# A two-layer graph convolution on one core: blocks of nodes that begin at the node of a fixed edge, and own rows moved at row numbers from registers

## The chip, the cores and the metric

The kernel runs on one core of a Trainium2 chip. TensorE (PE in the profile) multiplies, VectorE (DVE) and ScalarE (ACT) work on elements, GpSimd (POOL) issues the indirect DMAs, and SyncE (SP) issues all other DMAs. The metric is the time of one execution in microseconds (us); lower is better.

## The reference

There are N = 6250 nodes with D = 512 features each and E = 100000 edges, sorted by destination. With h = relu(layer_norm(x)):

```python
deg  = segment_sum(1, src)
dinv = where(deg > 0, 1 / sqrt(deg), 0)
conv(h, W0, W1, b) = h @ W0 + segment_sum(h[src] * (-dinv[src] * dinv[dst]), dst) @ W1 + b
h1  = conv(relu(layer_norm(x)), W1_0, W1_1, b1)
h1  = leaky_relu(layer_norm(h1, gamma, beta), 0.01)
out = x + conv(h1, W2_0, W2_1, b2)
```

All is float32. The costly part is the sum over edges: for each edge a row of 2 KB is fetched by its source's number, and the rows are added up by destination.

## The kernel before, in words

**Start.** The node rows (49 blocks of 128, the last one of 106) are loaded in eight groups. DVE makes one-hot tables of the source numbers (L215), PE counts them (L221), and this gives each node's degree and dinv. From the layer norm's statistics and dinv come scales (`sc`, L260 and L261); ACT (L270) and DVE (L266, L268) turn the rows into dinv * relu(layer_norm(x)), and eight stores on SP's queue write them to a table in DRAM, `tab[0]` (L272). The edges' numbers are turned on PE so that a chunk of 128 edges is a column: `sidx` holds the sources as integers in SBUF (L287), `dl` the destinations as floats in PSUM (L283).

**Main part (`usual_path`).** PE's and POOL's orders are written out by hand; the other engines' orders come from a scheduler. Two layers run one after the other. POOL's only work is `gather` (L315): one indirect DMA per chunk fetches the 128 source rows into one of R = 44 ring slots `zr`. There are 782 chunks, so 782 gathers a layer. A gather waits until the slot's last reader, 44 chunks back, is done, and until the gather eight before it has landed; each block's gathers stand in POOL's order before that block's other work, up to 44 chunks beyond the block's first.

For each block of 128 nodes:

- `own` (L326) loads the block's own rows `xt` from x by SP; in layer 0 ACT makes h from them with the columns `rs_all` and `nb_all`, in layer 1 h is loaded from `h_tab`. PE turns h (`hT`) and multiplies it by W0 (`start_products`).
- `sums` (L349) does the sum over edges. The edges are sorted but where a node's edges begin is not known when the program is built. So `chunk_ranges` gives each quarter of 32 nodes a range of chunks wide enough for the spread of the edges' positions, up to 12 chunks. DVE compares the chunks' destinations with the nodes (`sel`, one instruction, L367), and PE multiplies each chunk's 128x32 selection with its gathered rows (L378). The four quarters write to four groups of 32 columns of the array and run side by side: one step `s` of the loop over four quarters is called a round here. The profile counts two PE instructions for each of these products. The blocks of a layer have 544 rounds and 2170 products.
- ACT scales the sums by -dinv (`agg`, L381), PE turns them (L322) and multiplies by W1 (L439).
- `finish` (L384): in layer 0 a layer norm and the leaky relu, and stores of dinv * h1 to `tab[1]` (L409) and of h1 to `h_tab` (L413); in layer 1 the sum with x and the store to out (L391).

Layer 1's first gather waits for all stores to `tab[1]`. In layer 0 ACT also counts the edges that the selections hold (`held`, `n_seen`, L370). If at the end some edge was not seen, `general_path` computes all anew in another way; with the inputs used here all 100000 edges are seen, and it does not run.

The program prints here the functions that the change touches:

Of the kernel before, what the change touches and what calls it, by code (L numbers as in the profile page):

```python
# [8 lines left out]
F32 = mybir.dt.float32  # L9
# [7 lines left out]
POOL = mybir.EngineType.Pool  # L17

P = 128
# [3 lines left out]
LOADED = 8  # L23
# [10 lines left out]
def chunk_ranges(N, E):  # L34


    NC = -(-E // P)
    res = []
    for b in range(-(-N // P)):
        ends = [min(N, b * P + q * Q) for q in range(NQ + 1)]  # L40
        m = max(math.ceil(SPREAD * math.sqrt(E * (n / N) * (1 - n / N)) / P) for n in ends)
        res.append([(max(0, ends[q] * E // (N * P) - m),
                     min(NC, -(-ends[q + 1] * E // (N * P)) + m)) for q in range(NQ)])
    return res
# [3 lines left out]
def gnn_kernel(  # L48
# [26 lines left out]

    nc = tc.nc
# [10 lines left out]
    ranges = chunk_ranges(N, E)  # L87
    NK = max(hi - lo for r in ranges for lo, hi in r)
# [9 lines left out]
    tab = [dram.tile([NB * P, D], F32, name=f"tab{i}") for i in range(2)]  # L98
    h_tab = dram.tile([NB * P, D], F32, name="h_tab")
# [7 lines left out]
    sdinv = const.tile([P, NB], F32, name="sdinv")  # L107
    rs_all = const.tile([P, NB], F32, name="rs_all")
    nb_all = const.tile([P, NB], F32, name="nb_all")
# [5 lines left out]
    n_seen = const.tile([P, NQ * NB], F32, name="n_seen")  # L115
# [9 lines left out]
    nc.sync.dma_start(src_i, src.rearrange("(p j) -> p j", j=EJ))  # L125

# [54 lines left out]
    nc.gpsimd.memset(n_seen, 0.0)  # L181


    nm_all = ep.tile([P, NB], F32, name="nm_all")
# [54 lines left out]
    with tc.tile_pool(name="fold", bufs=1) as dp, tc.tile_pool(  # L239
        name="fold_ps", bufs=1, space=bass.MemoryType.PSUM  # L240
    ) as dps:
        deg = dps.tile([P, NB], F32, name="deg")
        each = ident.rearrange("k (n s) -> k s n", s=2)
        for t in range(2):
            for i in range(2):
                nc.tensor.matmul(deg[t * LO : (t + 1) * LO, :], each[:, i, :], both[:, :, t, i],
                                 start=(i == 0), stop=(i == 1))
        root = dp.tile([P, NB], F32, name="root")
        some = dp.tile([P, NB], F32, name="some")
        nc.vector.tensor_scalar_max(root, deg, 1.0)  # L250
        nc.scalar.activation(root, root, AF.Sqrt)
        nc.vector.tensor_single_scalar(some, deg, 0.0, op=OP.is_gt)
        nc.vector.reciprocal(root, root)
        nc.vector.tensor_mul(dinv, root, some)
        nc.vector.tensor_scalar_mul(ndinv, dinv, -1.0)
        nc.vector.tensor_scalar_mul(sdinv, dinv, SLOPE)


        sc = dp.tile([P, 2, NB], F32, name="sc")
        nc.vector.tensor_mul(sc[:, 0, :], rs_all, dinv)  # L260
        nc.vector.tensor_mul(sc[:, 1, :], nb_all, dinv)  # L261
        for (i0, n), t in zip(groups, xs):
            for j in range(n):
                i = i0 + j
                if i % 2:
                    nc.vector.tensor_scalar(t[:, j, :], t[:, j, :], sc[:, 0, i : i + 1], sc[:, 1, i : i + 1],  # L266
                                            op0=OP.mult, op1=OP.add)
                    nc.vector.tensor_scalar_max(t[:, j, :], t[:, j, :], 0.0)  # L268
                else:
                    nc.scalar.activation(t[:, j, :], t[:, j, :], AF.Relu, bias=sc[:, 1, i : i + 1],  # L270
                                         scale=sc[:, 0, i : i + 1])
            nc.sync.dma_start(tab[0][i0 * P : (i0 + n) * P, :].rearrange("(i p) d -> p i d", p=P), t)  # L272


    with tc.tile_pool(name="turn", bufs=1) as wp, tc.tile_pool(
        name="turn_ps", bufs=2, space=bass.MemoryType.PSUM
    ) as wps:
        for t, res in zip(chunks, (dl, sidx)):
            f = wp.tile([P, NG, P], F32, name="f", bufs=2)
            nc.vector.tensor_copy(f, t)  # L280
            for g in range(NG):
                if res is dl:
                    nc.tensor.transpose(dl[:, g * P : (g + 1) * P], f[:, g, :], ident)  # L283
                else:
                    fT = wps.tile([P, P], F32, name="fT")
                    nc.tensor.transpose(fT, f[:, g, :], ident)
                    nc.scalar.activation(sidx[:, g * P : (g + 1) * P], fT, AF.Copy)  # L287
# [4 lines left out]
    n_unseen = nc.values_load(unseen[0:1, 0:1], min_val=0, max_val=E,  # L292
                              skip_runtime_bounds_check_because="a count of edges")
# [5 lines left out]
def usual_path(tc, have):  # L299
    nc = tc.nc  # L300
    (x, out, rows, tab, h_tab, sidx, dl, iota_r, w_sb, ident, eps, ones, dinv, ndinv, sdinv, rs_all, nb_all,
     bias1, bias2, gam, bet, n_seen, unseen, ranges, NK, N, E, D, NB, NC, KD) = (
        have[n] for n in ("x out rows tab h_tab sidx dl iota_r w_sb ident eps ones dinv ndinv sdinv rs_all "
                          "nb_all bias1 bias2 gam bet n_seen unseen ranges NK N E D NB NC KD").split())
    R = 44
    with ExitStack() as es:
# [5 lines left out]
        seen = 0  # L312
# [13 lines left out]
        def own(layer, b):  # L326

            r = rows[b]
            xt = pool.tile([P, D], F32, name="xt")
            if r < P:  # L330
                nc.vector.memset(xt, 0.0)
            for lo, hi in parts(r):
                nc.sync.dma_start(xt[lo:hi], x[b * P + lo : b * P + hi, :])
            h = pool.tile([P, D], F32, name="h")
            if layer == 0:
                nc.scalar.activation(h, xt, AF.Relu, bias=nb_all[:, b : b + 1], scale=rs_all[:, b : b + 1])  # L336
            else:
                nc.sync.dma_start(h, h_tab[b * P : (b + 1) * P, :])
            ps, hT = transposed(h, "hT")
            nc.scalar.activation(hT, ps, AF.Copy)  # L340
            if layer == 1 and b == NB - 1:
                nc.vector.tensor_add(xt, xt, bias2)
# [6 lines left out]
        def sums(layer, b):  # L349
            nonlocal seen  # L350
            rng = ranges[b]
            sel = pool.tile([P, NQ, NK, Q], F32, name="sel")
            node = pool.tile([P, NQ, Q], F32, name="node")
            nc.scalar.activation(node, iota_r.rearrange("p (q c) -> p q c", c=Q), AF.Copy, bias=float(b * P))
            n = rng[0][1] - rng[0][0]
            step = rng[1][0] - rng[0][0]
            if all(rng[q] == (rng[0][0] + q * step, rng[0][1] + q * step) for q in range(NQ)):
                dl0 = dl[:, rng[0][0] : rng[0][0] + 1]
                parts = [(sel[:, :, :n, :], node[:, :, None, :].to_broadcast([P, NQ, n, Q]),
                          bass.AP(tensor=dl0.tensor, offset=dl0.offset,  # L360
                                  ap=[dl0.ap[0], [step, NQ], [1, n], [0, Q]]))]
            else:
                parts = [(sel[:, q, : hi - lo, :], node[:, q, None, :].to_broadcast([P, hi - lo, Q]),
                          dl[:, lo:hi, None].to_broadcast([P, hi - lo, Q]))
                         for q, (lo, hi) in enumerate(rng)]
            for o, i, d in parts:
                nc.vector.tensor_tensor(o, d, i, op=OP.is_equal)  # L367
                if layer == 0:
                    held = pool.tile([P, NQ, NK, Q], BF, name="held")
                    nc.scalar.activation(held[:, : o.shape[1], : o.shape[2]] if len(o.shape) == 4  # L370
                                         else held[:, 0, : o.shape[1], :], o, AF.Copy,
                                         accum_out=n_seen[:, seen : seen + 1])
                    seen += 1
            ps = psum.tile([P, D], F32, name="ps")
            for s in range(NK):
                for q, (lo, hi) in enumerate(rng):
                    if lo + s < hi:
                        nc.tensor.matmul(ps[q * Q : (q + 1) * Q, :], sel[:, q, s, :], zr[(lo + s) % R],  # L378
                                         start=(s == 0), stop=(lo + s == hi - 1))
            agg = pool.tile([P, D], F32, name="agg")  # L380
            nc.scalar.activation(agg, ps, AF.Copy, scale=ndinv[:, b : b + 1])  # L381
            return agg

        def finish(layer, b, v, xt):  # L384
            if layer == 1:
                o = pool.tile([P, D], F32, name="o")
                if b < NB - 1:
                    nc.vector.tensor_add(v, v, bias2)  # L388
                nc.vector.tensor_add(o, v, xt)  # L389
                for lo, hi in parts(rows[b]):  # L390
                    nc.sync.dma_start(out[b * P + lo : b * P + hi, :], o[lo:hi])  # L391
# [13 lines left out]
            di = dinv[:, b : b + 1]  # L405
            t = pool.tile([P, D], F32, name="t")
            nc.scalar.activation(t, v, AF.Copy, scale=sdinv[:, b : b + 1])  # L407
            nc.vector.scalar_tensor_tensor(t, v, di, t, op0=OP.mult, op1=OP.max)  # L408
            nc.sync.dma_start(tab[1][b * P : (b + 1) * P, :], t)  # L409
# [3 lines left out]
            nc.sync.dma_start(h_tab[b * P : (b + 1) * P, :], g)  # L413

        for layer in range(2):
            w0, w1 = w_sb[2 * layer + 1], w_sb[2 * layer]
            t = 0
            for b in range(NB):
# [9 lines left out]
                if b + 1 < NB:  # L428
                    next_xt, hT = own(layer, b + 1)
                agg = sums(layer, b)  # L430
                if b + 1 < NB:
# [4 lines left out]
                if b + 1 < NB:  # L436
# [5 lines left out]
            if layer == 0:  # L442
# [4 lines left out]
                nc.vector.tensor_scalar(unseen, all_ps[0:1, 0, 0:1], -1.0, float(E), op0=OP.mult, op1=OP.add)  # L447
# [318 lines left out]
```

## Time and profile before

| | before |
|---|---|
| median of 10 runs | 2125.45 us (2124.57 to 2128.2) |
| the profiled execution's own time | 2125.43 us |
| its span | 2123.6 us |
| PE busy | 1912.3 us (90%) |
| POOL busy | 1481.9 us (70%) |
| DVE, ACT busy | 622.6 us, 413.8 us |
| gathers (L315) | 1564, mean 946 ns |
| mean granted TensorE clock | 0.977 |
| mean DMA rate | 245 GB/s |

The profile is one execution. It lists groups of instructions with their busy time, the mean of one and the engine's idle time before them, with what ended it; the waits between engines; the instructions in order of time; and, for any stretch of time, each engine's busy time, the granted clock of PE and the share of time that the 16 DMA engines were busy. An engine can be busy most of the time and still not be what sets the end.

### The profile page before, as it was taken

The numbers are of one execution on the slowest core, as the hardware profiler recorded it, in microseconds if no ns is written. First come the engines' busy times: TensorE is split into PE (matmuls) and PEld (weight loads), VectorE is DVE, ScalarE is ACT, GpSimd is POOL, SyncE is SP. The second block draws the span as 40 slices with busy tenths as digits, with TensorE's granted clock in tenths as the row PEclk, the third lists the DMA queues.
The fourth block names the chain that finished last, engine by engine and source line by source line (L and its number), as shares of the span: only waits on it lengthen the run. The fifth ranks groups of instructions, "written<-read, shape, count | busy, mean of one in ns | idle before, by whom it ended". The sixth has DMA issues, their size and how long they took to land. (4 is left out here: it accounts for less than half of the span.)

```text
span 2123.6 us, 28647 instructions
## 1 busy us (share of the span) xinstructions
PE 1912.3 (90%) x11456; PEld 698.3 (33%) x11456; DVE 622.6 (29%) x824; ACT 413.8 (19%) x811; POOL 1481.9 (70%) x1577
## 2 busy tenths in 40 slices
PE   4358999999999999999886989999999999999896
PEld 4222333333333333333321323333333333333332
DVE  8913333333333333333231211111111112112111
ACT  8622222222222222222210000000000000000000
POOL 0047777777777777777756777777777777777774
PEclk9869999999999999999997999999999999999999
DMA  9488788888888888887866788788788787887884
GB/s 328 153 281 255 240 255 247 248 254 247 249 256 245 251 254 244 252 255 242 252 211 206 238 256 255 240 256 250 246 255 252 243 256 243 252 255 244 251 250 146
DMA packets 184811, 521.08 MB, mean 245 GB/s; under 512 B 30235, under 2 KB 31797, under 8 KB 184666
## 3 DMA queue, kind: packets, MB, share of 16 engines
q0 software_dynamic: 125120, 410.09, 64.4%
q1 hardware_dynamic: 59546, 109.04, 14.3%
q8 instruction: 92, 1.51, 0.3%
q14 instruction: 53, 0.43, 0.1%
HBM read 467.68 MB, written 51.34 MB: 244 GB/s over the span
## 5 line engine op out<-in xcount | busy, mean ns | idle before, releaser
L315 POOL DMA_INDIRECT zr<-tab,sidx x1564 | 1478.9, 946 | 617.8 <-issue 264.5
L378 PE MATMUL ps<-zr,sel 128*32 128x512 f32 x8680 | 1091.5, 602 | 113.8 <-DMA zr<-tab,sidx 109.6
L378 PEld LDWEIGHTS ps<-zr,sel 128*32 128x32 f32 x8680 | 280.8, 110 | 853.2 <-issue 449.7
L367 DVE TENSOR_TENSOR sel<-dl,node 128x1536 f32<-128x1536 f32 (+5 forms) x110 | 160.8, 1471 | 883.8 <-PE ps L378 866.3
L347 PE MATMUL u_ps<-w,hT 128*128 128x512 f32 x784 | 380.4, 608 | 1.8 <-ACT hT L340 1.8
L439 PE MATMUL u_ps<-w,aT 128*128 128x512 f32 x784 | 354.3, 595 | 1.6 <-DVE aT L435 1.6
L381 ACT ACTIVATE agg<-ps,ndinv 128x512 f32<-128x512 f32 x98 | 67.3, 687 | 937.5 <-PE ps L378 937.5
L439 PEld LDWEIGHTS u_ps<-w,aT 128*128 128x128 f32 x784 | 149.4, 191 | 189.7 <-issue 187.4
L347 PEld LDWEIGHTS u_ps<-w,hT 128*128 128x128 f32 x784 | 134.1, 191 | 178.7 <-issue 176.3
L340 ACT ACTIVATE hT<-hT_ps 128x512 f32<-128x512 f32 x98 | 58.5, 597 | 503.1 <-PE hT_ps L322 503.0
L393 DVE TENSOR_TENSOR u_ps<-u_ps,bias 128x512 f32<-128x512 f32 x49 | 34.3, 699 | 217.7 <-PE u_ps L439 217.7
L388 DVE TENSOR_TENSOR u_ps<-u_ps,bias 128x512 f32<-128x512 f32 x48 | 33.6, 699 | 214.1 <-PE u_ps L439 214.1
L435 DVE COPY aT<-aT_ps 128x512 f32<-128x512 f32 x98 | 67.7, 691 | 79.0 <-PE aT_ps L322 79.0
L370 ACT ACTIVATE held<-sel 128x1536 bf16<-128x1536 f32 (+5 forms) x55 | 68.9, 1254 | 46.9 <-DVE sel L367 46.9
L221 PE MATMUL both_ps<-hi,lo 125*128 125x196 bf16 x400 | 39.3, 254 | 42.8 <-DVE hi L215 42.7
L322 PE MATMUL hT_ps<-ident,h 128*128 128x128 f32 x392 | 59.3, 274 | 16.6 <-ACT h L336 16.6
L322 PEld LDWEIGHTS hT_ps<-ident,h 128*128 128x128 f32 x392 | 49.2, 142 | 67.5 <-issue 67.5
L322 PEld LDWEIGHTS aT_ps<-ident,agg 128*128 128x128 f32 x392 | 48.9, 141 | 54.2 <-issue 50.4
L322 PE MATMUL aT_ps<-ident,agg 128*128 128x128 f32 x392 | 58.9, 273 | 1.7 <-ACT agg L381 1.7
L221 PEld LDWEIGHTS <-lo 125*128 125x128 bf16 x400 | 35.9, 100 | 46.0 <-issue 34.4
L408 DVE SCALAR_TENSOR_TENSOR t<-u_ps,dinv,t 128x512 f32<-128x512 f32 x49 | 36.8, 750 | 37.0 <-ACT t L407 37.0
L407 ACT ACTIVATE t<-u_ps,sdinv 128x512 f32<-128x512 f32 x49 | 33.7, 687 | 64.1 <-DVE u_ps L403 64.1
(74 smaller groups left out, 531.6 us busy)
## 6 DMA issues: line engine op xcount, KB each, us to landing
zr<-tab,sidx POOLq DMA_INDIRECT x1564
xt<-in_x_dram SPq DMA_DIRECT2D x96, 256.0 KB
tab<-t SPq DMA_DIRECT2D x49, 256.0 KB
h_tab<-g SPq DMA_DIRECT2D x49, 256.0 KB
h<-h_tab SPq DMA_DIRECT2D x49, 256.0 KB
out_dram<-o SPq DMA_DIRECT2D x48, 256.0 KB
tab<-xs SPq DMA_DIRECT2D x6, 1792.0 KB
xs<-in_x_dram SPq DMA_DIRECT2D x5, 1792.0 KB
```

Source lines behind the costliest of these rows:

```text
L221: nc.tensor.matmul(both_ps, hot[0][:, j, :], hot[1][:, j, :], start=(g == 0 and j == 0), stop=(g == EJ // (2 * GJ) - 1 and j == GJ - 1))
L315: nc.gpsimd.indirect_dma_start(out=zr[t % R], out_offset=None, in_=tab[layer], in_offset=bass.IndirectOffsetOnAxis(ap=sidx[:, t : t + 1], ...
L322: nc.tensor.transpose(ps[:, kc, :], h[:, kc * P : (kc + 1) * P], ident)
L340: nc.scalar.activation(hT, ps, AF.Copy)
L347: nc.tensor.matmul(u_ps, hT[:, kc, :], w0[:, kc, :], start=(kc == 0), stop=False)
L367: nc.vector.tensor_tensor(o, d, i, op=OP.is_equal)
L370: nc.scalar.activation(held[:, : o.shape[1], : o.shape[2]] if len(o.shape) == 4 else held[:, 0, : o.shape[1], :], o, AF.Copy, accum_out=n_ ...
L378: nc.tensor.matmul(ps[q * Q : (q + 1) * Q, :], sel[:, q, s, :], zr[(lo + s) % R], start=(s == 0), stop=(lo + s == hi - 1))
L381: nc.scalar.activation(agg, ps, AF.Copy, scale=ndinv[:, b : b + 1])
L408: nc.vector.scalar_tensor_tensor(t, v, di, t, op0=OP.mult, op1=OP.max)
L435: nc.vector.tensor_copy(aT, aT_ps)
L439: nc.tensor.matmul(u_ps, aT[:, kc, :], w1[:, kc, :], start=False, stop=(kc == KD - 1))
```

## The change

Blocks of a layer no longer begin at multiples of 128 nodes. `block_plan` chooses a fixed step of 1888 edges; block b begins at the node after that of edge b * 1888 - 1, read from dst at run time (`begin_i`, one DMA of 51 single numbers), the first at node 0, the last at node N - 128. So a block's edges lie at chunk numbers known far better, and a quarter's range is 4 to 7 chunks where it was up to 12. There are 53 blocks instead of 49, with 357 rounds and 1246 products a layer instead of 544 and 2170. A block loads, computes and stores 128 rows; those from the next block's begin on (`owned`, 106 to 128 rows are its own with the inputs used here) get no sums and are overwritten by the next block, whose stores come later. All 100000 edges are again seen.

As a block's rows begin anywhere, the per-node scales are no longer columns in SBUF: rs, nb and dinv are turned on PE, copied by ACT (`all_sb`) and stored to a table `scales` in DRAM, and each block in layer 0 loads its 128x3 scales as single 4-byte numbers (`sb`) and DVE makes two more from them (`sn`). Own rows, h, the scales and all stores are moved at row numbers that SP loads into registers, eight blocks at a time (`values_load_multi_w_load_instructions`). The selection is made by four compares, one a quarter, against `node`, which one ACT and one DVE instruction make from `first` and `owned`. `astray` counts blocks that own fewer than 0 or more than 128 nodes.

The diff, cut to its core:

```diff
+    n = math.ceil((E - deg * P) / (deg * P - SPREAD * sd(P)))
+    step = 16 * math.ceil((E - deg * P) / (16 * n))
...
+    tab = [dram.tile([n, D], F32, name=f"tab{i}") for i, n in enumerate((NB * P, N))]
+    h_tab = dram.tile([N, D], F32, name="h_tab")
+    scales = dram.tile([3, NB * P], F32, name="scales")
...
+    nc.sync.dma_start(begin_i[:, 1 : BL - 1],
+                      bass.AP(tensor=dst.tensor, offset=dst.offset + step - 1, ap=[[1, 1], [step, BL - 2]]))
...
+    all3 = ep.tile([P, 3, NB], F32, name="all3")
+    rs_all, nb_all = all3[:, 0, :], all3[:, 1, :]
...
-        nc.vector.tensor_scalar_mul(sdinv, dinv, SLOPE)
+        nc.vector.tensor_copy(all3[:, 2, :], dinv)
...
+    nc.vector.tensor_scalar(begin[:, 1 : BL - 1], begin_i[:, 1 : BL - 1], 1.0, float(N - P), op0=OP.add, op1=OP.min)
...
+    nc.vector.tensor_copy(first_i, begin[:, :BL])
+        nc.tensor.matmul(first_ps, ones[0:1, :], begin, start=True, stop=True)
+        nc.vector.tensor_scalar_add(first, first_ps, 1.0)
+        all_ps = fps.tile([NB, 3, P], F32, name="all_ps")
+        for k in range(3):
+            nc.tensor.transpose(all_ps[:, k, :], all3[:, k, :], ident)
+        all_sb = ep.tile([NB, 3, P], F32, name="all_sb")
+        nc.scalar.activation(all_sb, all_ps, AF.Copy)
+        nc.sync.dma_start(scales.rearrange("k (b p) -> b k p", p=P), all_sb)
+    nc.vector.tensor_sub(owned, first[:, 1:], first[:, :BL])
...
 def own(layer, b):
+            if b % LOADED == 0:
+                n = min(LOADED, BL - b)
+                _, vals = nc.values_load_multi_w_load_instructions(
+                    first_i[0:1, b : b + n], engines=(SP,), min_val=0, max_val=N - P,
+                    skip_runtime_bounds_check_because="held to the last block above")
+                for k in range(n):
+                    row[b + k] = bass.ds(vals[k], P)
-            for lo, hi in parts(r):
-                nc.sync.dma_start(xt[lo:hi], x[b * P + lo : b * P + hi, :])
+            nc.sync.dma_start(xt, x[row[b], :])
             if layer == 0:
-                nc.scalar.activation(h, xt, AF.Relu, bias=nb_all[:, b : b + 1], scale=rs_all[:, b : b + 1])
+                nc.sync.dma_start(sb[:, b, :], scales[:, row[b]].rearrange("k p -> p k"))
+                nc.vector.tensor_tensor(sn[:, b, :], sb[:, b, 2:3].to_broadcast([P, 2]), signs, op=OP.mult)
+                nc.scalar.activation(h, xt, AF.Relu, bias=sb[:, b, 1:2], scale=sb[:, b, 0:1])
             else:
-                nc.sync.dma_start(h, h_tab[b * P : (b + 1) * P, :])
+                nc.sync.dma_start(h, h_tab[row[b], :])
...
 def sums(layer, b):
+            nc.scalar.activation(plain, iota_r, AF.Identity, bias=first[:, b : b + 1])
+            nc.vector.scalar_tensor_tensor(node, iota_r, owned[:, b : b + 1], plain, op0=OP.is_lt, op1=OP.mult)
+            for q, (lo, hi) in enumerate(rng):
+                wide = [P, hi - lo, Q]
+                nc.vector.tensor_tensor(sel[:, at[q] : at[q + 1], :], dl[:, lo:hi, None].to_broadcast(wide),
+                                        node[:, None, q * Q : (q + 1) * Q].to_broadcast(wide), op=OP.is_equal)
...
-            for s in range(NK):
+            for s in range(max(hi - lo for lo, hi in rng)):
                 for q, (lo, hi) in enumerate(rng):
                     if lo + s < hi:
-                        nc.tensor.matmul(ps[q * Q : (q + 1) * Q, :], sel[:, q, s, :], zr[(lo + s) % R],
+                        nc.tensor.matmul(ps[q * Q : (q + 1) * Q, :], sel[:, at[q] + s, :], zr[(lo + s) % R],
                                          start=(s == 0), stop=(lo + s == hi - 1))
-            nc.scalar.activation(agg, ps, AF.Copy, scale=ndinv[:, b : b + 1])
+            nc.scalar.activation(agg, ps, AF.Copy, scale=sn[:, b, 0:1])
...
 def finish(layer, b, v, xt):
-                for lo, hi in parts(rows[b]):
-                    nc.sync.dma_start(out[b * P + lo : b * P + hi, :], o[lo:hi])
+                nc.sync.dma_start(out[row[b], :], o)
...
-            nc.sync.dma_start(tab[1][b * P : (b + 1) * P, :], t)
+            nc.sync.dma_start(tab[1][row[b], :], t)
...
-            nc.sync.dma_start(h_tab[b * P : (b + 1) * P, :], g)
+            nc.sync.dma_start(h_tab[row[b], :], g)
```

In the built program the row-number DMAs keep their places in SP's order, each with a register instruction ahead of it; the two DVE instructions on `begin` and `first_i` stand before the first one-hot table, the copy `all_sb` stands on ACT ahead of the scaling of the rows, the store to `scales` stands on SP behind the eight stores to `tab[0]`, and the first gather waits for it too, because its ring slots reuse the memory of `all_sb`. POOL's order of gathers is the same.

## The prediction

> **What bounds the kernel now.** I read the page's first and fifth parts first: PE is busy 90% of the span, and its largest group, the rounds of L378, is what the change cuts.
>
> ```profile
> PE 1912.3 (90%) x11456; PEld 698.3 (33%) x11456; DVE 622.6 (29%) x824; ACT 413.8 (19%) x811; POOL 1481.9 (70%) x1577
> ...
> L315 POOL DMA_INDIRECT zr<-tab,sidx x1564 | 1478.9, 946 | 617.8 <-issue 264.5
> L378 PE MATMUL ps<-zr,sel 128*32 128x512 f32 x8680 | 1091.5, 602 | 113.8 <-DMA zr<-tab,sidx 109.6
> ```
>
> Then I asked whether the other candidate, POOL, ever rests. In the view of stretches of time, for L315 alone (busy us, count, PE's clock, DMA share, GB/s), each full 100 us holds the same work:
>
> ```profile
> 220.00:320.00 100.00, 75.63 (x81) 1.00 0.81 250
> 1000.00:1100.00 100.00, 75.62 (x81) 1.00 0.82 250
> 1600.00:1700.00 100.00, 75.63 (x81) 1.00 0.80 250
> ```
>
> 75.63 / 0.946 is 79.9 gathers in 100 us: one every 1.251 us, 0.946 busy and 0.30 between. The view of waits says the same (us in total, times, longest):
>
> ```profile
> PEld ps L378 <- DMA zr<-tab,sidx: 391.6, 431, 5.8
> POOL zr L315 <- issue: 264.5, 868, 0.3
> ...
> POOL zr L315 <- DMA zr<-tab,sidx: 134.6, 442, 0.3
> ...
> POOL zr L315 <- PE ps L378: 60.6, 199, 0.3
> ```
>
> Whatever POOL is said to wait for, it waits 0.3 us and never longer. The ring's first gathers, issued when PE does nothing, keep the same pitch. PE waits for the gathers, up to 5.8 us at a time. So the gathers' issue is the bound, and PE only nearly another. The span is a sum of five pieces: start to 125.27; 782 gathers, 781 x 1.251 = 977 us, to 1101.81; a turn between the layers of 21.16 us to 1122.97; 976 us to 2099.29; and the end, 24.3 us. 125.3 + 976.5 + 21.2 + 976.3 + 24.3 = 2123.6, the span. Its own time, 2125.43, is 1.8 us more, and the median is 2125.45.
>
> So only start, turn and end can move the span. In order of time (start, us, engine), the turn's first gather, then the end:
>
> ```profile
> 1122.97 0.94 POOL L315 DMA_INDIRECT zr<-tab,sidx  x1 [20.22 <-DMA tab<-t]
> ```
>
> ```profile
> 2099.29 0.95 POOL L315 DMA_INDIRECT zr<-tab,sidx  x1 [0.30 <-issue]
> ...
> 2102.31 1.07 PE L378 MATMUL ps<-zr,sel 128*32 128x512 f32 x8 [0.41 <-DMA zr<-tab,sidx]
> 2103.89 3.64 PE L378 MATMUL ps<-zr,sel 128*32 128x512 f32 x26 [0.52 <-DMA zr<-tab,sidx]
> ...
> 2109.83 5.40 PE L439 MATMUL u_ps<-w,aT 128*128 128x512 f32 x8 [0.79 <-DVE aT L435]
> ```
>
> and the start, where the scaled rows are stored:
>
> ```profile
> 87.14 17.74 ACT L270 ACTIVATE xs<-xs,sc 128x512 f32<-128x512 f32 x25 [1.21 <-DVE sc L261]
> ...
> 88.55 22.78 SPq L272 DMA_DIRECT2D tab<-xs  x8
> ```
>
> **The change part by part.** *The gathers* stay 2 x 782, in the same order: 0. Their cover against PE: a block now has 6.74 rounds (357 / 53). Products run in groups of up to four quarters, two passes each, 0.43 us a pass (the end's 26 instructions are one group of four and three of three: 8 passes in 3.64 us with the last one's full 0.59). So a round is 0.86 us, and a block's four other PE groups take (380.4 + 354.3 + 59.3 + 58.9) / 98 = 8.70 us. 6.74 x 0.86 + 8.70 = 14.5 us, against 782 / 53 x 1.251 = 18.46 us of gathers. The 374 rounds removed and the 8 block visits added (374 x 0.86 - 8 x 8.70 = 252 us of PE) lie beside POOL and buy nothing, unless at the ends.
>
> *DVE and ACT per block.* Four compares of 800 elements in all, by the rows of 1024 (1.223 us) and 256 (0.415): 0.146 + 1.05 ns an element, so 1.43 us against 1.76 now; two small ones (under 0.4) and one more ACT copy (0.3, as L354's). Both engines are idle for over half of a block: 0. DVE's `sn` waits for `sb`, with that block's compares behind it, but SP issues `sb` blocks ahead, right behind `xt`; at the start six `sn` stand ahead of the third block's compares, which PE needs some 35 us after the first gather. SP's extra DMA (0.32 us) and register instructions a block have 18 us: 0.
>
> *Own rows.* Three times 256 KB a block, 39 GB/s in a block's 20 us, become 8% more: 0. Layer 1's first h loads must now wait for the last `h_tab` store, as any row may be in it. Behind them stand PE's first transposes, and the round that needs chunk 11, which is issued 13.8 us after layer 1's first gather. Store, load (some 2 us each, as 1120.16 to 1122.97) and 8 products at half clock fit: 0.
>
> *The narrow loads.* `sb` is 384 numbers a block, 24 for each DMA engine. The trace has no 4-byte data. At 37.4 to 41 us mostly 512-byte packets kept all engines busy at some 42 ns each; the gathers' packets take 175 ns (64.4% of 16 engines over 125120). At 42 ns, 1.0 us an engine; at 175, 4.2. Of 18.46 us 19% is idle, 3.5 us. So 0 at 42, the nearest size, and (4.2 - 3.5) x 53 = +37 at 175, which I keep as a rival. The Trainium skill, "DMA: Bandwidth & Descriptors", Specifications, speaks against this load: below 512 bytes a DMA does read-modify-write. It gives no price per number, so by it the sum lies somewhere between my two ends; no row here shows it.
>
> *Start.* (a) Two DVE instructions stand ahead of the one-hot chain; small ones take 0.15 to 0.18 us: +0.3. If DVE has to wait for the 51 numbers, all 40 one-hots queue behind: up to +1.5. (b) ACT must copy `all_sb` before its 25 scalings, and that waits for three transposes. Four at half clock took 1.08 us (as at 127.93), a copy of 512 elements 0.60: 0.8 + 0.45, less 0.1 that the last `sc` took beside it: +1.15, between 0.5 and 2. The eight stores wait for these scalings, and DMA is full from 92 to 122 us (share 1.03), so they shift whole. (c) The first gather waits for the `scales` store too, 147 rows of 512 bytes: 0.4 us if spread over 16 engines, 6 on one; the load of 125 rows at 1 to 3 us kept only two tenths of the engines busy, so I take 21 rows on an engine, 0.85. Sum +2.3, bounds +0.9 and +9.
>
> *The turn and the end.* After chunk 781 lands, its group and three more ran, 3.64 us, as the last block's quarters ranged over 8, 8, 8 and 4 chunks. Now they range over 7, 7, 6 and 6: the group that holds chunk 781 holds the last two other products, and none follows. A lone group takes 1.07 (the row of 8 instructions). -2.57, twice. The out store of the block before, issued at 2098.57, moved beside the last gathers (4.60 us from issue to use; 3.85 at the turn, where no store did). It now comes some 1 us earlier: -0.2 (0 to -0.75). At the turn, the block before now ends its sums earlier and its store to `tab[1]` meets the last gathers: +0.6 (0 to +0.75, the difference of the two landings). Layer 1's first gather waits on three semaphores for ten: -0.1 (0 to -0.6).
>
> *The clock.* PE drops to half for 3.41 us after a stretch that it was half idle (busy us of PE first, clock behind the bracketed numbers):
>
> ```profile
> 2106.80:2110.21 3.41, 1.77 (x11) 0.72 (x6) 0.69 (x1) 0.69 (x1) 0.00 (x0) 1.00 0.01 2
> 2110.21:2113.62 3.41, 3.41 (x5) 1.33 (x4) 0.00 (x0) 0.00 (x0) 0.00 (x0) 0.50 0.02 7
> ```
>
> That cost the end 5.40 - 3.65 = 1.75 us, the turn nothing. With 4 us idle a block, PE will drop more often; one such stretch costs 1.7 us of PE, inside the 4. At each end I keep what is there: 0, bounds -1.75 and +1.75. The Trainium skill's "TensorE: Matmul & The Clock Gate", Part 1, names an idle window of about 3.4 us as the condition; the row shows a drop after a window 52% busy. By the page the end would run at full clock, 1.75 less, a sum of 2121.1; I go by the row.
>
> Sum: start +2.3; turn -2.57 + 0.6 - 0.1; end -2.57 - 0.2; in all -2.5. 2125.4 - 2.5 = **2122.9 us**.
>
> **The rivals.** *PE was the bound* (faster). For it: 90% busy. Then the 252 us would go, 1873. Against it: 0.3 us is POOL's longest wait for PE. Chance 0.02.
>
> *The ends gain more* (faster by over 4.25 us): the start costs only 0.9, the end keeps its clock, no store meets a gather: 0.9 - 5.14 - 0.6 - 0.75 - 1.75 = -7.3 at most, 2118.1; from 1.8 us below my sum on it decides. Chance 0.16.
>
> *The start delays more* (slower): the `scales` store on few engines, or a late `begin_i`; it decides from a start of +9.1 on, which my upper bounds just reach: 9.5 - 4.8 = +4.7, 2130.1. Chance 0.07.
>
> *The narrow loads fill the DMA engines* (slower). A gather waits for the one eight back, 10 us; landings take 3.9 to 4.6 now. Above 146 ns a number (3.5 / 24) the engines lack time and gathers come late: at 175 ns +37, 2161. Chance 0.05. That the blocks fail to cover the edges is excluded by the inputs.
>
> **How the numbers follow.** The likeliest case, the sum within 4.25 us of before, has 0.70; 0.2%, 4.25 us, is about what a measurement of this kernel tells from no change. Faster 0.16 + 0.02 = 0.18; slower 0.07 + 0.05 = 0.12; same 0.70. The range takes in the low end of the ends' case, 2118.5, and the start's, 2131; outside are PE as the bound, the narrow loads, and a little of both.
>
> **What would show it.** Right: L315 still 75.6 us in each 100; first gather near 127.5; turn near 19.1 us; PE busy some 80%, with a lower clock. Wrong: a pitch under 1.25 us, a POOL wait of over 0.3 us for gathers or PE within a layer, a first gather past 131.

## The result and the profile after

The changed kernel takes 2439.04 us (median of 9 runs, 2429.36 to 2453.12) against 2125.45 before: a ratio of 1.1482, 95% interval 1.1467 to 1.1497. It is slower, where no change to speak of was forecast. Its profiled execution took 2454.21 us, span 2452.4, so that all sums below go by 2452.4 against 2123.6, +328.8.

The page of the kernel after, first and fifth part:

```profile
PE 1714.8 (70%) x7957; PEld 628.1 (26%) x7957; DVE 652.5 (27%) x1353; ACT 420.7 (17%) x848; POOL 1483.2 (60%) x1578
...
L373 POOL DMA_INDIRECT zr<-tab,sidx x1564 | 1480.4, 947 | 913.1 <-PE ps L432 374.4
L432 PE MATMUL ps<-zr,sel 128*32 128x512 f32 x4984 | 789.5, 698 | 153.1 <-DMA zr<-tab,sidx 150.6
...
L380 PE MATMUL hT_ps<-ident,h 128*128 128x128 f32 x424 | 89.4, 350 | 479.1 <-DMA h<-h_tab 460.7
```

PE's rounds shrank as planned (1091.5 to 789.5 us busy), yet POOL's share of the span fell from 70% to 60%: it now rests. The last line is new: PE stood idle for 460.7 us ahead of the first transposes of a block, waiting for the load of h. Stretches of 100 us for the gathers alone (busy us, count, PE's clock, DMA share, GB/s) show where:

```profile
220.00:320.00 100.00, 75.62 (x81) 0.97 0.84 256
...
1600.00:1700.00 100.00, 56.29 (x60) 0.83 0.62 187
```

Layer 0 keeps the 75.6 us of before. Layer 1 does not. The five pieces of the span are: start to 125.89 (+0.6); layer 0's gathers 977.5 (+1.0); the turn 22.6 (+1.5); layer 1's gathers, 1126.00 to 2395.99, 1270.0 (**+293.7**); the end 56.4 (**+32.1**). The view of waits names the link (us in total, times, longest):

```profile
PE hT_ps L380 <- DMA h<-h_tab: 460.7, 52, 11.0
POOL zr L373 <- PE ps L432: 374.4, 269, 9.1
```

52 of the 53 blocks of layer 1, the layer in which h is loaded from DRAM, wait for it. PE falls behind, the ring of 44 chunks fills, and POOL waits for a free slot up to 9.1 us at a time. The chain that ended last, in one block of layer 1 (start, us, what):

```profile
1511.35 5.63 DMA h<-h_tab
...
1517.12 1.09 PE hT_ps L380 x4
1518.21 8.65 PE ps L432 x48
1526.86 1.91 PE u_ps L410 x4
...
1530.93 3.45 PE u_ps L491 x8
...
1534.40 0.71 DVE u_ps L442
...
1535.14 0.70 DVE o L443
...
1535.86 0.36 SPq L444
...
1536.40 0.33 SPq L394
...
1536.97 5.03 DMA h<-h_tab
```

It is a closed loop: the load of h, PE's whole block, the two DVE instructions that make o, then SP: the store of o (L444), the load of xt (L394), and next the load of h (issued at 1536.97) for the block that PE is already waiting for. Over the layer a turn of it takes 1270.0 / 53 = 23.96 us, against 18.46 us of gathers. In the kernel before, the same place in order of time (start, us, engine, line):

```profile
1520.61 0.60 PE L322 MATMUL hT_ps<-ident,h 128*128 128x128 f32 x4
...
1521.24 0.32 SPq L338 DMA_DIRECT2D h<-h_tab  x1
...
1521.55 0.69 DVE L389 TENSOR_TENSOR o<-u_ps,xt 128x512 f32<-128x512 f32 x1
...
1522.27 0.34 SPq L391 DMA_DIRECT2D out_dram<-o  x1
...
1522.65 0.43 SPq L333 DMA_DIRECT2D xt<-in_x_dram  x1
```

There the load of h went out as soon as PE had turned the h of two blocks before and freed its tile, ahead of the store of o, and had two blocks of time to land.

Only the orders of PE and POOL are written out by hand; SP's is made when the kernel is built. SP's queue in layer 1, per block, reads before: h(b+4), store of block b, xt(b+2); after: store of block b, xt(b+2), h(b+2). xt(b+2) needs the tile of xt(b), which the sum o(b) reads, and h stands behind it. The remark in the section on the change, that the row-number DMAs keep their places in SP's order, does not hold for these loads: h lost its place ahead of the store.

### The profile page after: what moved, and what is told of

The parts are those of the page before. It is cut to its first block, busy times and chain, and to the rows that moved or that the text cites. A ratio compares the mean times of both kernels' runs of the same rounds, so it can differ in the third digit from the quotient of the medians.

```text
span 2452.4 us, 22996 instructions
## 1 busy us (share of the span) xinstructions
PE 1714.8 (70%) x7957; PEld 628.1 (26%) x7957; DVE 652.5 (27%) x1353; ACT 420.7 (17%) x848; POOL 1483.2 (60%) x1578
## 3 DMA queue, kind: packets, MB, share of 16 engines
q0 software_dynamic: 125120, 410.09, 56.4%
## 4 chain that ended last, share of the span: by engine, by line
PE 43%; DMA 32%; POOL 8%; issue 8%; DVE 7%; SPq 2%; ACT 0%; POOLq 0%; DVEq 0%; ACTq 0%
PE ps L432 21%; DMA zr<-tab,sidx 19%; DMA h<-h_tab 12%; PE u_ps L410 10%; PE u_ps L491 9%; POOL zr L373 8%; PE hT_ps L380 2%; DVE o L443 1%; DVE u_ps L442 1%; PE aT_ps L380 1%; DVE lo L248 1%; SPq L394 1%; SPq L444 1%; DVE hi L248 1%; DMA scales<-all_sb 1%
## 5 line engine op out<-in xcount | busy, mean ns | idle before, releaser
L432 PE MATMUL ps<-zr,sel 128*32 128x512 f32 x4984 | 789.5, 698 | 153.1 <-DMA zr<-tab,sidx 150.6
L410 PE MATMUL u_ps<-w,hT 128*128 128x512 f32 x848 | 412.7, 610 | 30.3 <-DVE g L464 29.0
L380 PE MATMUL hT_ps<-ident,h 128*128 128x128 f32 x424 | 89.4, 350 | 479.1 <-DMA h<-h_tab 460.7
L422 DVE TENSOR_TENSOR sel<-dl,node 128x192 f32<-128x192 f32 (+3 forms) x424 | 122.2, 345 | 1017.6 <-PE ps L432 1017.4
L491 PE MATMUL u_ps<-w,aT 128*128 128x512 f32 x848 | 386.0, 598 | 1.6 <-DVE aT L487 1.6
L432 PEld LDWEIGHTS ps<-zr,sel 128*32 128x32 f32 x4984 | 165.9, 124 | 707.3 <-DMA zr<-tab,sidx 357.4
L435 ACT ACTIVATE agg<-ps,sn 128x512 f32<-128x512 f32 x106 | 72.9, 687 | 656.7 <-PE ps L432 656.7
L418 ACT ACTIVATE plain<-iota_r,first 128x128 f32<-128x128 f32 x106 | 41.5, 394 | 57.8 <-DVE node L419 44.5
L426 ACT ACTIVATE held<-sel 128x736 bf16<-128x736 f32 (+5 forms) x53 | 44.0, 831 | 41.3 <-DVE sel L422 41.3
L460 DVE SCALAR_TENSOR_TENSOR t<-u_ps,sb,t 128x512 f32<-128x512 f32 x53 | 39.8, 750 | 40.1 <-ACT t L459 39.3
L459 ACT ACTIVATE t<-u_ps,sn 128x512 f32<-128x512 f32 x53 | 36.4, 687 | 68.6 <-DVE u_ps L456 68.6
```

The costliest lines, as they stand in the source:

```text
L380: nc.tensor.transpose(ps[:, kc, :], h[:, kc * P : (kc + 1) * P], ident)
L410: nc.tensor.matmul(u_ps, hT[:, kc, :], w0[:, kc, :], start=(kc == 0), stop=False)
L422: nc.vector.tensor_tensor(sel[:, at[q] : at[q + 1], :], dl[:, lo:hi, None].to_broadcast(wide), node[:, None, q * Q : (q + 1) * Q].to_broad ...
L426: nc.scalar.activation(held[:, : at[NQ], :], sel[:, : at[NQ], :], AF.Copy, accum_out=n_seen[:, b : b + 1])
L432: nc.tensor.matmul(ps[q * Q : (q + 1) * Q, :], sel[:, at[q] + s, :], zr[(lo + s) % R], start=(s == 0), stop=(lo + s == hi - 1))
L435: nc.scalar.activation(agg, ps, AF.Copy, scale=sn[:, b, 0:1])
```

## The experiments

Theory 1: the place of the h load in SP's queue closes the loop. Theory 2: the shorter sums leave PE idle, its granted clock falls (0.82 from 1400 to 1700 us, against 1.00), and PE at that clock is the bound. Theory 3: register row numbers, narrow loads or the four more blocks cost too much in themselves.

**Two statements swapped.** In `own`:

```
+            h = pool.tile([P, D], F32, name="h")
+            if layer == 1:
+                nc.sync.dma_start(h, h_tab[row[b], :])
             xt = pool.tile([P, D], F32, name="xt")
             nc.sync.dma_start(xt, x[row[b], :])
-            h = pool.tile([P, D], F32, name="h")
...
-                nc.sync.dma_start(h, h_tab[row[b], :])
```

> The kernel after, with two statements in the other order: in layer 1 the load of h stands ahead of the load of xt for the same block, nothing else. SP's queue in layer 1 is then h(b+3) behind the store of block b instead of h(b+2), so a block's h load is issued one whole block (some 14 us of PE work) before PE wants it. Theory 1 (the h load is issued only after the store of the block two before, and its 5.6 us lie on PE's path, a closed loop of about 24 us per block): the loop opens, layer 1 goes back to the gathers' pitch, 782 x 1.251 = 978 us, PE waits for h under 0.5 us per block, and the whole is 125.9 + 977.5 + 22.6 + 978 + 21 to 25 + 1.8 = 2127 (2120 to 2134). Theory 2 (the shorter sums leave PE idle, the granted clock falls to 0.82 and PE at that clock is too slow): sums and clock stay as they are, so layer 1 stays above 1200 us and the whole above 2350. Theory 3 (register row numbers, narrow loads or the four more blocks cost SP or the DMA engines too much): all of them stay, 2440 within 20.

Measured: 2121.85 us (2120.14 to 2125.53, 11 runs) against 2126.74 of before on the same chip, ratio 0.9977 (0.9968 to 0.9986). All of the loss is gone. SP in one block of layer 1, with PE's next eight products behind it:

```profile
1526.32 0.36 SPq L446 DMA_DIRECT2D out_dram<-o  x1
...
1526.89 0.33 SPq L397 DMA_DIRECT2D xt<-in_x_dram  x1
...
1527.76 0.34 SPq L395 DMA_DIRECT2D h<-h_tab  x1
...
1541.48 3.60 PE L493 MATMUL u_ps<-w,aT 128*128 128x512 f32 x8
```

The load still follows the store, but it is now the load of a block later, and PE asks for it only behind the products that begin at 1541.48. The waits of POOL and PE:

```profile
POOL zr L373 <- PE ps L434: 61.8, 203, 0.3
...
PE hT_ps L380 <- DMA h<-h_tab: 12.1, 1, 12.1
```

One wait for h is left, at the turn, and within a layer POOL waits for 0.3 us at most again; layer 1 takes 976.9 us, and PE is busy 80% of the span. The clock from 1400 to 1700 us is 0.93 with the same short sums: theories 2 and 3 fall.

**More h tiles, same order.**

```
-            h = pool.tile([P, D], F32, name="h")
+            h = pool.tile([P, D], F32, name="h", bufs=4)
```

> The kernel after, with four h tiles instead of two, and the same order of SP's queue (h(b+2) behind the store of block b). Theory 1 (the place in SP's queue holds the load back, not the tile): no change, 2440 within 25, PE still waits 400 to 480 us for h in layer 1. A rival, that h has too few tiles to be loaded ahead: layer 1 back to 978 us and the whole near 2127.

Measured: 2448.5 us in one run; PE waits 463.3 us for h, 52 times. The tile was not what held it back.

**The cause alone, in the kernel before.**

```
+    first_i = const.tile([1, NB], I32, name="first_i")
+    nc.gpsimd.iota(first_i, pattern=[[P, NB]], base=0, channel_multiplier=0)
...
+            if b % 8 == 0 and b < NB - 1:
+                n = min(8, NB - 1 - b)
+                _, vals = nc.values_load_multi_w_load_instructions(
...
+                    row[b + k] = bass.ds(vals[k], P)
...
+            if r == P:
+                nc.sync.dma_start(xt, x[row[b], :])
...
-                nc.sync.dma_start(h, h_tab[b * P : (b + 1) * P, :])
+                nc.sync.dma_start(h, h_tab[row[b], :])
```

> The kernel before with one part of the change alone: xt and h of a block are loaded at a row number from a register (the same rows b x 128; the numbers written once at the start). Same blocks, same sums, no narrow loads, no scales. SP's queue in layer 1 changes from the h load of block b+5 ahead of the store of block b's next to h(b+2) behind the store of block b, as in the kernel after. Theory 1: per block 19.1 us of PE work at full clock, 1.4 DVE, 1.1 SP and 5.5 of the load in a closed loop, 27 to 30 us with the clock's drop after each wait: layer 1 49 x 28.5 = 1397 us, the whole 125.3 + 976.5 + 21.2 + 1397 + 40 = 2560 (2490 to 2650), slower than the kernel after. Theory 2 (short sums and the clock): sums are as long as before, so 2126 within 6. Theory 3 (narrow loads or four more blocks): neither is there, 2126 within 6; if the registers themselves cost SP, some 1 us per block at most, hidden.

Measured: 2496.02 us (2492.84 to 2499.24), ratio 1.1732 (1.1714 to 1.1750); layer 1 1329.6 us, 27.1 a block, the low end of the 27 to 30 expected. Its chain has the same loop with a longer sum in it:

```profile
1522.99 5.06 DMA h<-h_tab
...
1528.19 1.08 PE hT_ps L325 x4
1529.27 11.88 PE ps L392 x96
```

So the loss needs none of the new blocks, sums or scales. And inside the closed loop the shorter sums do count: 27.1 us a block here, 23.96 in the kernel after.

**Its control: h alone from a register.** As the last, with xt's rows written out:

```
-                nc.sync.dma_start(h, h_tab[b * P : (b + 1) * P, :])
+                nc.sync.dma_start(h, h_tab[row[b], :])
```

> The kernel before with only the h loads of layer 1 at a row number from a register (the same rows); xt keeps its rows written out. The same register loads and h loads as in the run in which both take the register, but SP's queue keeps the order of before: h(b+5) directly ahead of the store of block b+1. Theory 1 (the place in SP's queue is the cause): layer 1 stays at 976 us, the whole 2127 within 6. Rival (a transfer at a register's row number is itself slower or later): layer 1 longer by some us per block, the whole above 2300.

Measured: 2122.44 us, ratio 0.9987 (0.9977 to 0.9997), layer 1 977.3 us. SP in one block of layer 1:

```profile
1522.17 0.34 SPq L348 DMA_DIRECT2D h<-h_tab  x1
1523.19 0.34 SPq L401 DMA_DIRECT2D out_dram<-o  x1
1523.58 0.44 SPq L343 DMA_DIRECT2D xt<-in_x_dram  x1
```

So the load of h at a register's row number costs nothing here by itself; the order of SP's queue changed where both xt and h of a block took the register. (xt alone was not tried. In this profile the start is 1.7 us shorter than before, the turn 2.0 longer and the end 2.9 shorter, with the last eight products at 3.70 us for 5.40.)

**PE kept busy in the wait.**

```
+                if layer == 1 and b + 1 < BL:
+                    spare = psum.tile([P, KD, P], F32, name="hT_ps", bufs=1)
+                    for k in range(7):
+                        nc.tensor.matmul(spare.rearrange("p k c -> p (k c)"), ident, w1[:, k % KD, :],
+                                         start=(k == 0), stop=(k == 6))
```

> The kernel after with seven spare products of 128x512 on PE at the end of each block of layer 1, into a PSUM tile that nothing reads: 7 x 0.86 = 6.0 us at full clock, in the 8 to 9 us in which PE waits for h. The late load stays. Theory 1: the load still closes the loop; PE is granted more clock (over 0.9 in layer 1), so the loop loses only the slow part of its 15.5 us of PE work: 14.5 + 1.4 + 1.1 + 5.6 = 22.6 us, layer 1 53 x 22.6 = 1198 and the whole about 2367 (2340 to 2440). Theory 2 (the clock is the cause): with the clock back, layer 1 near 978 us and the whole near 2130.

Measured: 2423.18 us in one run; layer 1 1238.1 us, 23.36 a block. The stretch from 1400 to 1700 us of this kernel (PE, PEld, DVE, ACT and POOL busy with their counts, PE's clock, DMA share, GB/s):

```profile
1400.00:1700.00 300.00, 266.88 (x1037) 102.88 (x1035) 44.25 (x98) 20.24 (x36) 172.65 (x183) 0.93 0.63 192
```

The clock rose from 0.82 to 0.93, and in the two profiles this gave back 0.6 us of the 5.5 lost per block; as the runs of the changed kernel spread from 2429 to 2453 us, half a microsecond a block, one run of 2423 fixes this only to some 0.1 to 0.6. Theory 1's centre, 2367, was too hopeful: the load took 6.66 us, not 5.6, in the block looked at, and the transposes still took 1.09 us instead of 0.60. What the clock gave back is a tenth of the loss at most, and the low clock followed from the wait: without the wait, in the swapped kernel, it is 0.93 too.

**Another cure: more xt tiles.**

```
-            xt = pool.tile([P, D], F32, name="xt")
+            xt = pool.tile([P, D], F32, name="xt", bufs=4)
```

> The kernel after with four xt tiles instead of two, the statements in the order of after. SP's queue in layer 1 is then xt(b+4), h(b+4) behind the store of block b: the load of xt, which stands ahead of h, no longer has to wait for the sum that reads the xt of two blocks before. Theory 1: h is issued two blocks ahead, the loop opens, layer 1 at 977 us and the whole 2122 within 4, as with h ahead of xt. A rival, that it is h's standing behind xt as such (its own issue, 0.3 us, or the two transfers side by side) that costs: no change, near 2440.

Measured: 2120.89 us, ratio 0.9979 (0.9970 to 0.9988); one wait for h, 11.1 us at the turn. With the result of four h tiles this shows which wait held h back: that of xt for its tile, until o(b) was made.

**The narrow loads twice**, on top of the swap:

```
+                for _ in range(2):
                     nc.sync.dma_start(sb[:, b, :], scales[:, row[b]].rearrange("k p -> p k"))
```

> The kernel with h ahead of xt (2121.85) with each block's narrow load (128x3 numbers of 4 bytes) issued twice into the same place: 53 more of them, 20352 more packets of 4 bytes in layer 0. Theory: they lie beside the gathers' issue and nothing on the path waits for them, 0: 2122 within 2.5, layer 0 at 977 us from first to last gather. Rival (each number fills its DMA engine for 175 ns and pushes the gathers): about 37 us more in layer 0, 2159.

Measured: 2119.40 us, ratio 0.9975 (0.9965 to 0.9986), layer 0 977.4 us. That is 0.1 us below the range expected, on another chip than the swap, where before took 2.3 us less as well. Twice the narrow loads cost nothing that can be told.

**PE kept busy at the two ends**, on top of the swap: `fill(1)` is one product of 128x256 into the h transposes' PSUM tile.

```
+                if b == BL - 1 and s >= rounds - 3:
+                    fill(1)
...
+                if b == BL - 1:
+                    fill(1)
                 aT_ps, aT = transposed(agg, "aT")
+                if b == BL - 1:
+                    fill(1)
```

> The kernel with h ahead of xt (2121.85) with one spare product of 128x256 on PE (0.44 us at full clock, into a PSUM tile that nothing reads) before each of the last three rounds of the last block's sums in both layers, one between the sums and the transposes, and one between the transposes and the last eight products. Theory (PE's idle time just before the end lowers its clock, and the last 14 sums at 3.6 and the last eight products at 5.4 us are 2.0 to 2.8 us longer than at full clock): end from 22.0 to about 19.5 us, the turn, whose eight products already took 3.7 us there, unchanged; the whole 2119.5 (2117.5 to 2121). Rival (the spare products only push the real ones later): 0.5 to 2 us longer, 2123.

Measured: 2123.28 us, ratio 0.9995 (0.9986 to 1.0004), some 0.2% behind the swap alone. PE at the end, in order of time:

```profile
2107.13 0.70 PE L446 MATMUL hT_ps<-w,ident 128*128 128x256 f32 x2
2107.76 1.05 PE L437 MATMUL ps<-zr,sel 128*32 128x512 f32 x4
...
2111.10 3.70 PE L506 MATMUL u_ps<-w,aT 128*128 128x512 f32 x8 [0.35 <-DVE aT L502]
```

The last eight products took 3.70 us for 5.40 (whether by the spare ones is not shown: they took 3.70 in three of the profiles without them too, those of h alone from a register, of four xt tiles and of the doubled narrow loads). But each spare one stood in the way of real ones for some 0.6 us: the end fell from 22.0 only to 21.1 us, and the turn, which the expectation had left unchanged, rose from 19.05 to 20.84. The rival was right.

The best versions are thus the changed kernel with h loaded ahead of xt (0.9977), or with four xt tiles (0.9979); the intervals do not tell them apart. Their lead over the kernel before is 0.2%, and the kernel before with h alone from a register, which removes no work, came out at 0.9987; how much of so small a lead is due to the change is not shown.

## Why the prediction was wrong

The step that failed is *Own rows*: "Layer 1's first h loads must now wait for the last `h_tab` store ... fit: 0". It asked about the wait of the first loads only, and of those it was right: in the swapped kernel PE waits 12.1 us for h once, at the turn, and layer 1 keeps its pitch. Of all later loads it took for granted that SP would issue them ahead, as before, and beside it the step on DVE and ACT counted SP's time a block ("have 18 us: 0") but not its order. SP issues in order, and its view of waits was worth reading: before, SP stood longest at the load of h, waiting for PE to free its tile (868.5 us in 49 waits), and for o at the store of out only 100.3 us; in the kernel after it stands at that store, 1115.3 us in 53 waits. Such a wait is harmless in itself (778.9 us in the swapped kernel), but the load of h for block b+2, once it stands behind the store of block b, goes out when PE already wants it. The price, missing from the sum, was 293.7 us in layer 1 and the 32.1 at the end, where PE, behind by the ring, had just begun the sums of the third block from the last when the last gather went out. The sign that the prediction had named for its being wrong, a POOL wait of over 0.3 us for PE within a layer, is what came.

None of the four rivals covered this. New waits were looked for at the start, at the turn and in the narrow loads, not in the order of the queue that the change touched in every block. The estimate of "some 2 us" for a load came from the turn, where it about holds (first load of h issued at 1126.18, transposes at 1128.83 in the kernel after); beside the gathers the loads on the chain took 5.0 to 8.2 us in all but two cases, with a median of 5.8.

With that one order mended, the other steps can be read from the swapped kernel:

- *The gathers*: right. 977.0 and 976.9 us in the two layers (976.5 and 976.3 before), 1.251 us a gather; the PE work removed bought nothing there.
- *DVE and ACT*, 0: right. `sn` waits for `sb` 102.3 us in 52 waits in the kernel after, and layer 0 does not feel it.
- *The narrow loads*: right at 0, and the rival at 175 ns a number is excluded by doubling them. The Trainium skill's "DMA: Bandwidth & Descriptors", Specifications, warns of read-modify-write below 512 bytes; whatever it costs an engine here, no run shows it in the time.
- *Start*, +2.3: measured +0.6 (125.89). In (a) the wait for the source numbers ended at 6.74, not 7.78 us, which more than paid for the two small instructions; so in spite of `all_sb` (b, 0.48 us) the scalings began at 87.08 against 87.14; why that wait was shorter is not shown. In (c) the store of `scales` was done at 124.40, where the last table store had been done at 124.36. But in the two variants of the old kernel with registers, which store no `scales`, the table stores were done at 122.57 and 122.73, so that (c) may still hide 1.7 us. What is left, 0.6, was not in the sum: `plain` and `node` ahead of the first compare, 1.49 us from there to the first gather against 0.91.
- *The turn*, -2.07: right. 19.05 us with the swap, 19.43 with four xt tiles, against 21.16; the sums ended 5.3 us after the layer's last gather against 7.5. In the kernel after itself it was 22.6, mostly as the last eight products took 6.56 us (clock 0.50, then 0.61) for 3.70; with four h tiles, the same work up to there, they took 3.70 and the turn 19.9.
- *The end*, -2.77: 22.0 us with the swap against 24.3, -2.3, but by another way, so the size is luck. The last products did not shrink to one group of 1.07 us; they ran at a granted clock of 0.53:

```profile
2102.95 3.60 PE L434 MATMUL ps<-zr,sel 128*32 128x512 f32 x14 [1.21 <-DMA zr<-tab,sidx]
```

The sums so ended 7.7 us after the last gather against 8.2, and the last eight products took 5.40 us as before. The other 1.8 us came from a stretch that the sum did not have: from the issue of the last store to the end of the span, 5.8 us against 7.6. The kernel before stores its last block in two transfers, the changed one in one; whether that is the reason is not shown. With four xt tiles the last group took 1.06 us, as forecast, and the last eight products 3.70; the end was 18.8 us (19.3 with doubled narrow loads, where they took 3.70 as well). The clock's bound of 1.75 was the right size, and it falls either way from profile to profile.

- *The clock*: as said, PE drops more often, and within a layer this costs nothing while the gathers bind: 0.93 in the swapped kernel from 1400 to 1700 us against 1.00 before. "TensorE: Matmul & The Clock Gate", Part 1, of the Trainium skill ties the drop to an idle window of about 3.4 us. The closed loop, with waits of up to 11.0 us before a block's transposes, agrees: those then took 1.08 to 1.09 us instead of 0.60. The prediction's row, a drop after a window in which PE was 52% busy, does not, and the row decides.

In total the sum comes close for a kernel that differs from the one built in the order of two statements, but partly by luck. Its span is 2120.8 us against 2123.6, -2.8 where the sum had -2.5: the start +0.6 for +2.3, the gathers +1.1 for 0, the turn -2.1 for -2.07, the end -2.3 for -2.77. By the medians on one chip, 2121.85 against 2126.74, it is -4.9.

## What to carry to other kernels

When a change touches transfers, read each in-order queue transfer by transfer: what stands ahead of this load, what does that wait for, and who will ask for the load and when. A cover of 18 us a block is worth nothing to a load that is issued after its block should have begun. Where row numbers in registers make a builder keep loads in the order of the statements, as SP's order in these runs suggests, put the load that is wanted first, or whose tile comes free first, in front; here two swapped statements were worth 15% of the time of the kernel before.

## What the runs showed of the hardware that was not expected

The same eight stores of scaled rows, 12.8 MB in all, first issued at 88.5 to 89.0 us, were done at 124.36 us in the kernel before and at 122.57 and 122.73 in its two variants with row numbers from registers, although those began to scale 0.3 and 0.4 us later. The first gather went out at 125.27 in the one and at 123.45 and 123.61 in the others; in the changed kernel and its six variants it went out at 125.87 to 126.38. With one profile of each kernel it is not shown whether this is chance or belongs to the kernels. The 1.7 us are 0.08% of the time.

A load of 256 KB beside the gathers, at 62% of the DMA engines' time, took 5.8 us in the median and up to 8.2. In one loop with some 2.6 us of DVE and SP and, by subtraction from 23.96, some 15.5 us of PE, this made a single late load a block cost 15%.
